# A graph layer on one core: the hand-made order of instructions is given up for the framework's scheduler

## The chip, the cores and the metric

The kernel runs on one NeuronCore of a Trainium2 chip. The metric is the device time of one launch in microseconds (us): the median of three runs, 1224.73 us (1222.9 to 1227.51). Five engines work side by side, each through its own list of instructions in order: PE (TensorE, matmuls, with PEld for its weight loads), DVE (VectorE), ACT (ScalarE), POOL (GpSimd) and SP (SyncE, which here only issues transfers). ACT and POOL issue transfers too, from the same lists.

## The reference, cut to what matters

```python
edge_index = jnp.stack([src, dst])               # 100000 edges, sorted by dst; 6250 nodes of 128 features
Xs = X[src]
m_data = Xs @ W_data.T + b_data
m_ctrl = Xs @ W_control.T + b_control
msg = jnp.where((edge_types == 0)[:, None], m_data, m_ctrl)
agg = jax.ops.segment_sum(msg, dst, num_segments=X.shape[0])
out = jax.nn.relu(agg + (X @ W_self.T + b_self))
x = _layernorm(x + out, axis=-1)
```

## The kernel before, in words

The nodes are cut into 49 blocks of 128. `sums_over_windows` works in three stretches.

**Build** (`messages`, lines 270 to 302). Seven groups of seven blocks. A group's inputs come in one transfer `xt_sb` (line 276, 448 KB, issued by ACT, two buffers). Each block has one float32 matmul with the three weight matrices (line 284) and one that adds the bias (285), into one of three PSUM buffers `g_ps`. ACT and DVE split the two kinds of message into three bfloat16 parts each (lines 289, 291, 292; POOL makes the last, 293), and ACT copies the node's own term (290). At a group's end ACT issues the store of `own` (296) and two stores of `table` (299). The messages also stay in SBUF as `m3`.

**Places** (`place(grp)`, lines 377 to 555), once for each of six groups of five blocks. For 18 steps k DVE writes one-hot tiles `hot_st` (434, five instructions of 128 columns, nine buffers), PE counts with them (438, matrix `tri`), DVE reads the slot (441), PE closes the count (445, matrix `rest`); every third step DVE makes `hr` and `two` (415, 418) and PE scatters them (426). Then come short chains (469 to 554) and one POOL gather `msg_s` (538). The result is written to DRAM as `packed` (458) and read back, spread over all partitions, as `rows` (368), one for each block.

**Sums.** For 30 of the blocks, `packed_sums` (563 to 608) runs 25 ticks each. A tick is one quad, four matmuls of 32 weight columns each into `g_ps` (line 581; their weights are `rows`, made ready by DVE at 561); a one-hot `hot_p` from DVE (584, four buffers); a cast `gs` from ACT (587, four buffers); and, two ticks later (`LAG`), one matmul that adds the tick to `agg_p` (590). A block ends with one more matmul (594), four DVE steps on its sums (`finish`, 88 to 91), and each fifth block with the layer norm (`norm_and_store`, 99 to 129: some twenty DVE steps, one ACT square root, one store). For the other 19 blocks `gathered` (320 to 362) fetches each edge's message by POOL (337, six at a time, six buffers `msg`), DVE writes a one-hot `hot` (354, four buffers) and PE adds (355, `agg_g`); the end of a block is `finish` and, each fifth time, the layer norm.

What sets the order: `manual_schedule()` (line 148) keeps each engine's list in the order in which the program was written. That order is made by the driver at lines 611 to 637: `place(0)` is stepped three times for each build block from the 15th on; then each tick of `packed_sums` is followed by a step of the next `place`, and by as many steps of `gathered` as spread its 342 tiles over the 750 ticks. Buffers and the waits on them come from the tile pools in either case.

Of the kernel before, what the change touches and what calls it, by code (L numbers as in the profile page):

```python
# [46 lines left out]
def kernel(  # L47
# [83 lines left out]
    with ExitStack() as main:  # L131
        sums_over_windows(main, tc, x, xt, edges, w, bias, table, own, packed, total,
                          finish, load_rows, norm_and_store)
# [6 lines left out]
def sums_over_windows(ctx, tc, x, xt, edges, w, bias, table, own, packed, total,  # L140
# [4 lines left out]
    work = ctx.enter_context(tc.tile_pool(name="work", bufs=2))  # L145
    ps_g = ctx.enter_context(tc.tile_pool(name="ps_g", bufs=3, space=PSUM))
    ps_a = ctx.enter_context(tc.tile_pool(name="ps_a", bufs=1, space=PSUM))
    ctx.enter_context(tc.manual_schedule())


    r0 = const.tile([EC, 1], I32, name="r0")
# [597 lines left out]
```

## Time and profile before

| what | value |
|---|---|
| median of the runs | 1224.73 us |
| profiled execution, its own time | 1234.9 us |
| its span, first to last instruction | 1233.2 us |
| PE busy | 804.8 us (65%) |
| DVE busy | 664.2 us (54%) |
| ACT busy | 405.3 us (33%) |
| POOL busy | 371.7 us (30%) |
| mean granted clock of PE | 0.718 |

All terms further on come from the profiled execution, which is 0.8% above the median. A row of the profile names the line of the program, the engine, the operation, `out<-in` and the number of instructions; a bracket at its end is the time that the engine stood idle just before, and what released it. [...]

### The profile page before, as it was taken

The numbers are of one execution on the slowest core, as the hardware profiler recorded it, in microseconds if no ns is written. First come the engines' busy times: TensorE is split into PE (matmuls) and PEld (weight loads), VectorE is DVE, ScalarE is ACT, GpSimd is POOL, SyncE is SP. The second block draws the span as 40 slices with busy tenths as digits, with TensorE's granted clock in tenths as the row PEclk, the third lists the DMA queues.
The fourth block names the chain that finished last, engine by engine and source line by source line (L and its number), as shares of the span: only waits on it lengthen the run. The fifth ranks groups of instructions, "written<-read, shape, count | busy, mean of one in ns | idle before, by whom it ended". The sixth has DMA issues, their size and how long they took to land.

```text
span 1233.2 us, 16402 instructions
## 1 busy us (share of the span) xinstructions
PE 804.8 (65%) x5211; PEld 253.3 (21%) x5211; DVE 664.2 (54%) x2722; ACT 405.3 (33%) x921; POOL 371.7 (30%) x405
## 2 busy tenths in 40 slices
PE   4454454534777657677677766677776777567784
PEld 1111121101222112222122221222222222112221
DVE  3043440413665456666576655676657666544455
ACT  2211112212333333333343333334343334234462
POOL 2110111272333233243332334314333332233400
PEclk9555555556777578786697777868768787577896
DMA  2512204431111132112231121322123211232200
GB/s 53 148 30 75 75 7 128 154 105 44 59 60 41 65 119 67 49 45 86 87 102 54 39 76 40 107 74 66 43 77 115 74 61 28 78 108 81 83 1 21
DMA packets 72192, 86.87 MB, mean 70 GB/s; under 512 B 18534, under 2 KB 61843, under 8 KB 72051
## 3 DMA queue, kind: packets, MB, share of 16 engines
q0 software_dynamic: 16736, 34.26, 10.0%
q1 hardware_dynamic: 35054, 35.26, 8.9%
q10 hardware_dynamic: 20310, 16.26, 4.4%
q8 instruction: 41, 0.67, 0.2%
q14 instruction: 51, 0.42, 0.1%
HBM read 69.51 MB, written 16.23 MB: 70 GB/s over the span
## 4 chain that ended last, share of the span: by engine, by line
PE 32%; issue 27%; DVE 15%; POOL 14%; DMA 6%; another core or an unknown queue 2%; ACT 2%; ACTq 0%; POOLq 0%; DVEq 0%
POOL msg L337 14%; PE g_ps L581 9%; PE agg_p L590 9%; PE g_ps L284 5%; PE agg_g L355 4%; DMA xt_sb<-in_xt 4%; DVE hot_st L434 2%; PE g_ps L285 2%; PE acc L438 2%; DVE s L90 1%; DVE two L418 1%; DVE hot_p L584 1%; DMA msg<-table,idx 1%; DVE r L291 1%
## 5 line engine op out<-in xcount | busy, mean ns | idle before, releaser
L587 ACT CAST gs<-g_ps 128x384 bf16<-128x384 f32 (+1 forms) x750 | 351.9, 480 | 581.6 <-PE g_ps L581 408.4
L337 POOL DMA_INDIRECT msg<-table,idx x342 | 331.3, 969 | 536.1 <-PE agg_g L355 436.6
L590 PE MATMUL agg_p<-gs,hot_p 128*128 128x384 bf16 (+1 forms) x750 | 297.7, 397 | 124.2 <-issue 76.2
L584 DVE TENSOR_SCALAR hot_p<-iota_b,to 128x128 bf16<-128x128 bf16 (+1 forms) x750 | 188.9, 262 | 270.1 <-PE agg_p L590 120.7
L581 PE MATMUL g_ps<-m,rows 128*32 128x384 bf16 x2940 | 306.4, 399 | 6.2 <-DVE rows L561 6.2
L355 PE MATMUL agg_g<-msg,hot 128*128 128x384 bf16 x342 | 137.8, 406 | 137.9 <-DVE hot L354 107.2
L581 PEld LDWEIGHTS <-rows 128*32 128x32 bf16 x2940 | 78.7, 96 | 286.4 <-issue 276.6
L284 PE MATMUL g_ps<-w_sb,xt_sb 128*128 128x384 f32 x98 | 76.5, 883 | 60.0 <-DMA xt_sb<-in_xt 60.0
L434 DVE TENSOR_SCALAR hot_st<-iota_b,st 128x128 bf16<-128x128 bf16 x540 | 112.2, 266 | 0.0
L590 PEld LDWEIGHTS <-hot_p 128*128 128x128 bf16 (+1 forms) x750 | 73.5, 98 | 176.1 <-issue 172.3
L441 DVE TENSOR_REDUCE slot<-acc 128x5 f32<-128x490 f32 x108 | 71.9, 666 | 50.1 <-PE acc L438 32.3
L438 PE MATMUL acc<-hot_st,tri 128*128 128x490 bf16 x108 | 52.0, 481 | 65.0 <-DVE hot_st L434 56.3
L291 DVE TENSOR_TENSOR r<-g_ps,m 128x256 f32<-128x256 f32 x49 | 20.8, 424 | 134.0 <-ACT own_sb L290 134.0
L293 POOL TENSOR_TENSOR m<-r,m 128x256 bf16<-128x256 f32 x49 | 32.8, 669 | 194.2 <-ACT m L292 194.2
L354 DVE TENSOR_SCALAR hot<-iota_b,rel 128x128 bf16<-128x128 bf16 x342 | 88.0, 258 | 0.2
L355 PEld LDWEIGHTS <-hot 128*128 128x128 bf16 x342 | 35.6, 104 | 235.3 <-DVE hot L354 177.5
L289 ACT CAST m<-g_ps 128x256 bf16<-128x256 f32 x49 | 18.2, 372 | 143.5 <-PE g_ps L285 143.4
L561 DVE TENSOR_SCALAR rows<-rows,pid 128x800 bf16<-128x800 bf16 x120 | 50.2, 421 | 0.6 <-DMA xs<-in_x 0.6
L445 PE MATMUL acc<-hot_st,rest 128*128 128x490 bf16 x108 | 49.6, 460 | 1.1 <-DVE slot L441 1.1
L284 PEld LDWEIGHTS g_ps<-w_sb,xt_sb 128*128 128x128 f32 x98 | 25.4, 305 | 105.6 <-issue 90.3
L426 PEld LDWEIGHTS <-hot_st 128*128 128x128 bf16 x540 | 37.5, 113 | 42.3 <-issue 35.2
L426 PE MATMUL small<-two,hot_st 128*128 128x64 bf16 x540 | 41.0, 216 | 3.3 <-DVE two L418 3.3
(135 smaller groups left out, 376.8 us busy)
## 6 DMA issues: line engine op xcount, KB each, us to landing
rows<-packed SPq DMA_DIRECT2D x30, 784.0 KB
table<-m ACTq DMA_DIRECT2D x14, 672.0 KB
msg<-table,idx POOLq DMA_INDIRECT x342
xt_sb<-in_xt ACTq DMA_DIRECT2D x7, 448.0 KB
own<-own_sb ACTq DMA_DIRECT2D x7, 448.0 KB
xs<-in_x SPq DMA_DIRECT2D x49, 64.0 KB
xs<-own SPq DMA_DIRECT2D x49, 64.0 KB
out<-h_p SPq DMA_DIRECT2D x6, 320.0 KB
```

What stands on the lines that cost most here:

```text
L284: T.matmul(y, xt_sb[:, j, :], w_sb, start=True, stop=False)
L337: G.indirect_dma_start(out=msgs[c][:, k, :], out_offset=None, in_=table[:, :], in_offset=bass.IndirectOffsetOnAxis(ap=idx[:, j, k0 + k : k ...
L354: V.tensor_scalar(hot, iota_b, rel[:, j, k0 + k : k0 + k + 1], None, op0=ALU.is_equal)
L355: T.matmul(agg, hot, msg[:, k, :], start=k0 + k == 0, stop=k0 + k == KT - 1)
L426: T.matmul(vt_v[:, q, :], hots[k][:, q, :], two[:, k - k0, q, :], start=k == 0 and q == 0, stop=k == KT - 1, skip_group_check=True)
L434: V.tensor_scalar(hot[:, q, :], iota1_b, st1[:, q, k : k + 1], None, op0=ALU.is_equal)
L438: T.matmul(acc_v, tri, hot[:, :, :NT], start=k == 0, stop=False, skip_group_check=True)
L441: V.tensor_reduce(slot[:, k, :], acc_v, axis=AX.X, op=ALU.max)
L581: T.matmul(g_ps[t * R : (t + 1) * R, :], sp[:, 4 * g + t, :], m3[:, 4 * g + t, :], start=True, stop=True)
L584: V.tensor_scalar(hot[: n * R], iota_b[: n * R], to[: n * R, q, g : g + 1], None, op0=ALU.is_equal)
L587: A.copy(gs[: n * R], g_ps[: n * R])
L590: T.matmul(agg, hot[: n * R], gs[: n * R], start=g == 0, stop=False)
```

## The change

One line goes; everything else is the same word for word.

```diff
     ps_a = ctx.enter_context(tc.tile_pool(name="ps_a", bufs=1, space=PSUM))
-    ctx.enter_context(tc.manual_schedule())
+
```

The same instructions with the same buffers are now put in order by the framework's scheduler: it plays the program through with its own table of durations, and lets each engine take, of the instructions whose inputs and buffers it takes to be ready, the one that stands first in the program. The lists differ in many places; three of them follow. In each, the first fence is the order before and the second the order now.

ACT, at the end of the build's first group. `xt_sb` is the transfer of a later group's inputs; `m` is `m3`, `r` is `r1`.

```order
L289 CAST m_347<-g_ps 128x2x128
L290 COPY own_sb<-g_ps 128x128
L292 CAST m_347<-r_425 128x2x128
L296 DMA own<-own_sb 128x7x128
L299 DMA table<-m_347 128x7x384 x2
L276 DMA xt_sb<-in_xt 128x896
L289 CAST m_347<-g_ps 128x2x128
```

```order
L292 CAST m_345<-r_405 128x2x128
L276 DMA xt_sb<-in_xt 128x896
L292 CAST m_345<-r_414 128x2x128
L289 CAST m_345<-g_ps 128x2x128
L290 COPY own_sb<-g_ps 128x128
L289 CAST m_345<-g_ps 128x2x128
L296 DMA own<-own_sb 128x7x128
```

Before, the second group's inputs are asked for behind the first group's stores. Now the first two groups' inputs are asked for at the start (two of these transfers stand in a row there), and the one shown is the third group's, ahead of the first group's stores.

DVE, where the first five packed blocks are normalised (103 to 119); `hot_p` is what PE needs for the next ticks.

```order
L104 BN_AGGR mv<-st 128x2
L107 TENSOR_SCALAR v<-mv 128x5
L111 RECIPROCAL r_3322<-s_3320 128x5
L113 TENSOR_TENSOR q<-v,r_3322 128x5
L114 TENSOR_TENSOR q<-q,s_3320 128x5
L116 RECIPROCAL rstd<-q 128x5
L117 TENSOR_SCALAR rstd<-rstd 128x5
L119 TENSOR_SCALAR h_p<-h_p,mv,rstd 128x128 x5
```

```order
L103 BN_STATS st<-h_p 128x6
L584 TENSOR_SCALAR hot_p<-iota_b,to 128x128
L104 BN_AGGR mv<-st 128x2
L584 TENSOR_SCALAR hot_p<-iota_b,to 128x128
L107 TENSOR_SCALAR v<-mv 128x5
L88 TENSOR_TENSOR s<-agg_g,xs 128x128
L584 TENSOR_SCALAR hot_p<-iota_b,to 128x128
L90 TENSOR_TENSOR s<-agg_g,s 128x128
L111 RECIPROCAL r_3320<-s_3318 128x5
```

The layer norm was one piece of DVE's list; now one-hots for PE, and another block's `finish`, stand between its steps.

PE, in a packed block beside which the next `place` runs. A quad is the four matmuls of line 581, each with its weight load.

```order
L590 MATMUL agg_p<-gs,hot_p 128x384
L355 LDWEIGHTS hot
L355 MATMUL agg_g<-msg,hot 128x384
L581 LDWEIGHTS rows
L581 MATMUL g_ps<-m_347,rows 32x384
L581 LDWEIGHTS rows
L581 MATMUL g_ps<-m_347,rows 32x384
L581 LDWEIGHTS rows
L581 MATMUL g_ps<-m_347,rows 32x384
L581 LDWEIGHTS rows
L581 MATMUL g_ps<-m_347,rows 32x384
L590 LDWEIGHTS hot_p
```

```order
L590 MATMUL agg_p<-gs,hot_p 128x384
L581 LDWEIGHTS rows
L581 MATMUL g_ps<-m_345,rows 32x384
L355 LDWEIGHTS hot
L355 MATMUL agg_g<-msg,hot 128x384
L581 LDWEIGHTS rows
L581 MATMUL g_ps<-m_345,rows 32x384
L581 LDWEIGHTS rows
L581 MATMUL g_ps<-m_345,rows 32x384
L581 LDWEIGHTS rows
L581 MATMUL g_ps<-m_345,rows 32x384
L590 LDWEIGHTS hot_p
```

Before, all 750 quads stand in one piece. Now 177 of them are cut by another matmul (166 once and 11 twice: 188 cuts), nearly all in the sixth to the 25th packed block, some nine a block. Counted over a block, PE's work has kept its place: at each end of a packed block as many tiles of `gathered` and steps of `place` lie behind PE as before, within five or so. One shift is larger: ten of the 18 steps of `place(1)` now stand inside the build, beside those of `place(0)`. POOL's list is the same, within six gathers.

## Rows read from the trace of the kernel before

**Rows 1.** The page: busy time of each engine, share of the span, instructions.

```profile
PE 804.8 (65%) x5211; PEld 253.3 (21%) x5211; DVE 664.2 (54%) x2722; ACT 405.3 (33%) x921; POOL 371.7 (30%) x405
```

**Rows 2.** Stretches of the build: us, busy times, granted clock (PEclk), DMA share, GB/s.

```profile
40.20:54.50 14.30, 14.09 (x21) 4.19 (x21) 2.55 (x6) 5.73 (x19) 3.41 (x6) 0.50 0.19 34
65.50:97.50 32.00, 19.00 (x46) 6.53 (x47) 17.53 (x57) 6.62 (x21) 4.33 (x7) 0.50 0.01 3
105.90:139.00 33.10, 20.38 (x63) 7.64 (x63) 17.57 (x48) 5.67 (x18) 4.00 (x6) 0.50 0.00 0
```

**Rows 3.** The page's costliest groups: busy, mean ns; idle before and its releaser.

```profile
L284 PE MATMUL g_ps<-w_sb,xt_sb 128*128 128x384 f32 x98 | 76.5, 883 | 60.0 <-DMA xt_sb<-in_xt 60.0
```

**Rows 4.** The build in order of time: start, us, instruction, idle before.

```profile
16.90 1.62 PE L284 MATMUL g_ps<-w_sb,xt_sb 128*128 128x384 f32 x2 [2.93 <-DMA xt_sb<-in_xt]
...
26.74 0.91 PE L284 MATMUL g_ps<-w_sb,xt_sb 128*128 128x384 f32 x2
...
27.84 0.91 PE L284 MATMUL g_ps<-w_sb,xt_sb 128*128 128x384 f32 x2
...
33.05 1.46 ACTq L276 DMA_DIRECT2D xt_sb<-in_xt  x1
...
40.31 1.62 PE L284 MATMUL g_ps<-w_sb,xt_sb 128*128 128x384 f32 x2 [11.29 <-DMA xt_sb<-in_xt]
...
77.67 0.57 PE L438 MATMUL acc<-hot_st,tri 128*128 128x490 bf16 x1 [1.85 <-DVE hot_st L434]
```

**Rows 5.** Between build and sums, in order of time.

```profile
243.91 1.44 DVE L561 TENSOR_SCALAR rows<-rows,pid 128x800 bf16<-128x800 bf16 x4 [0.64 <-DMA xs<-in_x]
...
285.72 0.48 ACT L587 CAST gs<-g_ps 128x384 bf16<-128x384 f32 x1 [14.91 <-remote]
```

**Rows 6.** Packed blocks from one line 594 to the next; columns as in rows 2.

```profile
341.77:375.21 33.44, 26.05 (x173) 8.23 (x173) 22.67 (x89) 11.68 (x26) 12.05 (x12) 0.74 0.15 46
...
636.37:672.33 35.96, 26.02 (x173) 7.95 (x172) 21.71 (x86) 11.58 (x26) 11.33 (x12) 0.76 0.19 59
...
1151.86:1176.50 24.64, 18.60 (x137) 5.56 (x137) 11.40 (x49) 11.66 (x26) 8.22 (x9) 0.86 0.26 82
1176.50:1194.73 18.23, 16.01 (x136) 5.37 (x136) 11.06 (x48) 11.97 (x26) 0.00 (x0) 1.00 0.01 1
```

**Rows 7.** PE's waits from 300 to 1200 us: in total, times, longest.

```profile
PE agg_g L355 <- DVE hot L354: 100.7, 70, 9.0
...
PE acc L438 <- DVE hot_st L434: 17.2, 9, 4.0
...
PE agg_g L355 <- DVE bad L551: 7.5, 1, 7.5
```

**Rows 8.** The first layer norm: its last step, and PE behind it.

```profile
445.80 1.37 DVE L119 TENSOR_SCALAR h_p<-h_p,mv,rstd 128x128 f32<-128x128 f32 x5
...
447.77 0.50 PE L355 MATMUL agg_g<-msg,hot 128*128 128x384 bf16 x1 [8.80 <-DVE hot L354]
```

**Rows 9.** PE's matmuls at the lower clock, then at the full one.

```profile
449.52 0.50 PE L590 MATMUL agg_p<-gs,hot_p 128*128 128x384 bf16 x1
...
449.81 0.53 PE L355 MATMUL agg_g<-msg,hot 128*128 128x384 bf16 x1
...
450.27 0.51 PE L581 MATMUL g_ps<-m,rows 128*32 128x384 bf16 x4
...
450.71 0.50 PE L590 MATMUL agg_p<-gs,hot_p 128*128 128x384 bf16 x1
...
1207.23 0.34 PE L590 MATMUL agg_p<-gs,hot_p 128*128 128x384 bf16 x1
...
1207.40 0.33 PE L355 MATMUL agg_g<-msg,hot 128*128 128x384 bf16 x1
...
1207.66 0.35 PE L581 MATMUL g_ps<-m,rows 128*32 128x384 bf16 x4
...
1207.94 0.34 PE L590 MATMUL agg_p<-gs,hot_p 128*128 128x384 bf16 x1
```

## The prediction

> **What bounds the kernel now.** I read the busy times first: no engine is near its span, and PE is the fullest at 65% [rows 1]. So the question in each stretch is for what PE waits, and the views of PE's idle time come next.
>
> In the build PE waits for transfers: 60.0 us ahead of the float32 matmuls, all put down to `xt_sb` [rows 3]. One row shows why: the second group's inputs are issued at 33.05, behind the first group's stores, and PE starts at 40.31 after 11.29 us of idleness [rows 4]. A group without `place` beside it is solid: 14.09 us busy of 14.30, so 2.04 us a block at a granted clock of 0.50 [rows 2]. A group with `place` beside it lasts 32 to 33 us with 19 to 20 busy [rows 2]: 13 us go in handing over between PE and DVE, as in the 1.85 us for `hot_st` [rows 4].
>
> In the sums the views by packed block say most. A late block without `place` takes 24.64 us while POOL gathers and 18.23 when POOL is done [rows 6]: some 6.4 us of a block go with the gathers, whatever the order (in the first long burst a cast on ACT stood still for 14.91 us [rows 5]). With `place` beside it a block takes 33 to 36, and PE is busy for 26 [rows 6]. So in these blocks PE's own list, with a fifth of the time lost to the gathers, is what ends last; DVE has 22 us of work there. The waits of PE that an order can cure are those for DVE: 100.7 + 17.2 + 7.5 = 125.4 us [rows 7]. Seven of them, of 6.9 to 9.0 us (the longest 9.0 [rows 7]), stand at a layer norm and come to 56 us; the first, 8.80 us, ends as the normalisation's last steps are through [rows 8].
>
> **The change, part by part**, against the profiled execution's 1234.9 us (span 1233.2, 1.7 outside).
>
> *Transfers of the build.* Each group's inputs are now asked for while the group before is computed, 14 us or more for a transfer that takes 7 (33.05 to 40.31 [rows 4]). Of the 60.0 us the first wait, 2.93, before any work, stays [rows 4]: **-57**. The cover is a whole group on PE; if it were gone the 57 would be back.
>
> *`place` in the build.* Ten more steps k stand there. Two groups with six steps each have 19.00 and 20.38 us of PE against 14.09 in one without [rows 2], so 0.93 us a step: **+9**. The handovers cost 13 us in each of these groups (32.00 - 19.00, 33.10 - 20.38 [rows 2]) and the same in a third, 39 us for 18 steps or 2.2 a step. Now `hot_st` is written ahead, which takes most of the 1.85 us away, but 14 of the 28 counts have their second half right behind them and wait for DVE's reduction. I take 1.25 a step, 35 in place of 39: **-4**. Bounds: 62, if each of 28 steps kept 2.2; 14, if only the 14 waits of about a microsecond were left.
>
> So the build ends 52 us sooner. Behind it nothing is new: the last store, `rows`, its selection (first at 243.91 [rows 5]) and the 36 gathers follow each other as before.
>
> *Steps of `place(1)` gone from the sums.* A block with six steps takes 33.44, one without 24.64 [rows 6], so 1.47 us a step; ten: **-14**.
>
> *Layer norms.* With one-hots for PE between its steps, PE goes on while DVE normalises, though more slowly, since DVE's work is as much as before. I take three quarters of 56: **-42** (bounds -25 and -56).
>
> *Shorter waits for DVE.* 125.4 less 56 leaves 69 us, many of them short and behind a block's `finish`. `finish` too is now mixed with one-hots. I take a good third: **-26** (0 to -50).
>
> *Cut quads.* This is what the change costs. From one matmul of full width to the next PE goes in 0.29 us at the lower clock (449.52 to 449.81) and 0.17 at the full one (1207.23 to 1207.40); into a quad or out of it the step is 0.44 to 0.46 and 0.26 to 0.28 [rows 9]. In the order sum, tile, quad, sum this makes 0.29 + 0.46 + 0.44 = 1.19 us, or 0.71; in the order sum, one, tile, three, sum there are four steps into or out of a quad's width: 1.80, or 1.08. A cut costs 0.6 us at the lower clock and 0.37 at the full one. These blocks run at 0.74 to 0.76 [rows 6], half way, so 0.48; 188 cuts: 91 us. A quarter of it should fall into the time that the gathers take from PE anyway: **+68** (bounds +20, if most is hidden, and +113, all at the lower clock).
>
> [...]
>
> Sum: -57 + 9 - 4 - 14 - 42 - 26 + 68 = -66, so 1168.9 us in that execution. The median is 0.8% below the profiled one (1224.73 / 1234.9 = 0.992), which makes **1159 us**, 5% faster. With the bounds of the single terms moved against each other, this case reaches from 1115 to 1203.
>
> **Rivals**, in the same scale.
>
> *PE's clock rises in the build.* In the first group the float32 matmuls went from 1.62 to 0.91 us after ten microseconds of work, one block each 1.10 us [rows 4]; a later group, as solid and 14 us long, stayed at 0.50 [rows 2]. Without the pauses the full clock may come and stay: 42 blocks save up to 0.94 us each, less what ACT's casts then hold back, some 33 us: 1169 - 33 = 1136, so 1127. Against it: that second group. [...]
>
> *The cuts are hidden.* If PE is not what ends last in the blocks with `place`, a cut costs little: +20 in place of +68, 1121, so 1112. For it: PE is idle for 7 to 10 us in such a block [rows 6]. Against it: 6.4 of these go with the gathers.
>
> *The norms' waits come back.* DVE has the same work, and a one-hot that now stands behind some other late step makes PE wait in turn. If none of the 68 us (42 + 26) is gained, the sum is +2, 1237, and the time 1227: no change.
>
> *Slower.* The cut quads cost more than the slots. ACT casts a quad only when its fourth matmul is through, so a cut delays the cast (0.48 us long [rows 5]) and the sum that waits for it. The gains come to 134 us (57 - 9 + 4 + 14 + 42 + 26), so the change turns at 0.71 us a cut. At the lower clock a cut with the cast's length on top is 0.6 + 0.48 = 1.08; three quarters of 188 x 1.08 are 152, the sum is +18, 1253, so 1243. For it: casts and sums stand only two ticks apart, with three PSUM buffers. Against it: most quads stay whole in a third of the blocks, and two ticks are a microsecond or more.
>
> That the order does not change is excluded by the lists themselves.
>
> **How the numbers follow.** 0.5% is about what a measurement of this kernel can tell from no change: 6 us, from 1218.6 to 1230.9. Chances: forecast (1115 to 1203) 0.47; clock rises (1127) 0.15; cuts hidden (1112) 0.15; waits come back (1227) 0.09; slower (1243) 0.14. Faster 0.47 + 0.15 + 0.15 = 0.77, same 0.09, slower 0.14. The range goes from 1088, since the two fast rivals can meet, to 1232, which leaves out the slower case and a little at the low end.
>
> **What would show it.** Build: idle time for `xt_sb` near 3 us in place of 60, the first selection of `rows` near 192 us in place of 243.91 [rows 5], at a granted clock near 0.5 before it. Sums: PE's waits of over 6 us for `hot` gone, those for DVE together near 57 in place of 125; packed blocks with a norm at 32 to 34 us, the blocks from the sixth to the 25th without one 2 to 3 us longer than before, the first three near 25; the last six unchanged. The forecast is wrong if blocks with nine cuts take no longer, if they take over 5 us longer, or if that first selection moves by less than 35 or more than 75 us.

## The result, and the profile after

The changed kernel takes 1065.43 us (median; 1047.55 to 1071.72), the kernel before 1226.12 us beside it: a ratio of 0.859, with a 95% interval from 0.846 to 0.872, some 14% faster. The ratio leaves out two of the four runs, over 1.5% longer than the shortest, of which the profiled one is one; with them the medians give 0.869. The forecast was 1159 us with a range from 1088 to 1232, so the direction was right and the time lies below the range. The profiled execution took 1071.72 us.

First the page of the changed kernel: span, busy times, the granted clock in 40 slices.

```profile
span 1070.0 us, 16296 instructions
...
PE 794.8 (74%) x5211; PEld 255.0 (24%) x5211; DVE 623.9 (58%) x2722; ACT 397.0 (37%) x921; POOL 371.8 (35%) x405
...
PEclk9986555568867997886988869898688788588788
```

PE is busy for 795 us, 10 less than in [rows 1]. What fell is its idle time, from 428 us (1233.2 - 804.8) to 275. By stage, in the two traces, with the first selection of `rows` and the lines 594 as marks:

| stage | before | after | change |
|---|---|---|---|
| start to first selection of `rows` | 243.9 | 163.1 | -80.8 |
| from there to the end of the first packed block | 65.0 | 64.2 | -0.8 |
| the 29 other packed blocks | 903.6 | 829.1 | -74.5 |
| behind the last of them | 20.7 | 13.7 | -7.0 |

The forecast had -52 for the first row and -14 for the rest. The build as a whole, from its first float32 matmul to its last (columns as in rows 2), of the kernel before:

```profile
16.90:231.50 214.60, 115.78 (x275) 38.57 (x276) 69.27 (x188) 45.46 (x145) 31.60 (x48) 0.55 0.25 71
```

and of the changed one:

```profile
20.80:151.30 130.50, 117.95 (x341) 39.20 (x342) 90.98 (x289) 42.30 (x145) 32.06 (x47) 0.73 0.40 116
```

PE has 66 more matmuls there and is idle for 12.5 us in place of 98.8. The records of the granted clock, a share of full speed, hold two values in these two traces, 0.50 and 1.00. In the kernel before it is 0.50 from 447 to 452 us, where the first half of [rows 9] lies, and 1.00 from 1206 to 1208, where the second lies. The granted clock of the two rows here (0.55 and 0.73) does not show a rise. The clock's record begins only 26 us after the start in the first trace and 63 us in the second, and the profile counts what lies ahead of it as full clock, here and in PEclk. In the changed kernel:

```profile
20.80:63.00 42.20, 39.76 (x78) 12.35 (x79) 24.54 (x82) 12.99 (x45) 9.34 (x14) 1.00 0.40 111
```

and in that stretch the float32 matmuls of a block took

```profile
22.79 1.65 PE L284 MATMUL g_ps<-w_sb,xt_sb 128*128 128x384 f32 x2
```

which is their length at the lower level (1.62 us in [rows 4], where the other is 0.91). Of the 49 blocks of the build 4 took under 1 us for them, 3 in the kernel before: by these lengths the build ran at the lower clock both times, for the most part. The page's group that answers to [rows 3]:

```profile
L284 PE MATMUL g_ps<-w_sb,xt_sb 128*128 128x384 f32 x98 | 76.1, 878 | 5.2 <-DMA xt_sb<-in_xt 3.2 <-DVE r L291 2.0
```

The largest of PE's waits from 20.8 to 151.3 us:

```profile
PE acc L445 <- DVE slot L441: 9.6, 13, 1.0
```

In the sums the waits have changed their kind. PE's waits of the changed kernel over the whole span (in total, times, longest):

```profile
PE g_ps L581 <- ACT gs L587: 61.3, 54, 4.0
PE agg_p L590 <- ACT gs L587: 53.0, 29, 14.2
PE agg_p L590 <- issue: 48.4, 27, 11.0
PE g_ps L581 <- issue: 35.0, 32, 3.2
PE acc L445 <- DVE slot L441: 18.8, 24, 2.3
PE agg_p L590 <- DVE hot_p L584: 9.9, 11, 2.0
...
PE agg_g L355 <- DVE hot L354: 3.2, 4, 2.2
```

The 100.7 us for `hot` of [rows 7] are 3.2 now. In their place stand waits for casts and waits that the profile puts down to nothing, 198 us together against 137 before. One of them in order of time, ACT's row and then PE's:

```profile
217.99 0.48 ACT L587 CAST gs<-g_ps 128x384 bf16<-128x384 f32 x1 [14.92 <-remote]
...
218.52 0.48 PE L590 MATMUL agg_p<-gs,hot_p 128*128 128x384 bf16 x1 [14.16 <-ACT gs L587]
```

It is the kind of stall of [rows 5], in the first long burst of gathers, with PE behind it. These stalls turned out to be the main thing to understand in the experiments: with the kernel itself unchanged, they are there at some times and not at others. The kernels of one set were timed on one chip together with the kernel before, and every ratio below is against it: it took 1255 and 1258 us in two sets (and 1226 above), 1028 to 1032 us in four. Chip number 10 gave 1032 in one set and 1258 in another, so "a chip with the stalls", as the expectations say, should read "a set of runs with the stalls".

### The profile page after: what moved, and what is told of

The parts are those of the page before. It is cut to its first block, busy times and chain, and to the rows that moved or that the text cites. A ratio compares the mean times of both kernels' runs of the same rounds, so it can differ in the third digit from the quotient of the medians.

```text
span 1070.0 us, 16296 instructions
## 1 busy us (share of the span) xinstructions
PE 794.8 (74%) x5211; PEld 255.0 (24%) x5211; DVE 623.9 (58%) x2722; ACT 397.0 (37%) x921; POOL 371.8 (35%) x405
## 4 chain that ended last, share of the span: by engine, by line
PE 68%; another core or an unknown queue 10%; issue 7%; DVE 7%; ACT 5%; DMA 2%; ACTq 0%; DVEq 0%; SPq 0%
PE g_ps L581 25%; PE agg_p L590 19%; PE agg_g L355 7%; PE g_ps L284 6%; ACT gs L587 5%; PE acc L438 3%; PE acc L445 3%; PE small L426 2%; PE g_ps L285 2%; DVE slot L441 2%; DVE hot_st L434 1%; PE agg_p L594 1%; DVE hot_p L584 1%; DVE two L418 1%
## 5 line engine op out<-in xcount | busy, mean ns | idle before, releaser
L587 ACT CAST gs<-g_ps 128x384 bf16<-128x384 f32 (+1 forms) x750 | 347.0, 480 | 541.4 <-PE g_ps L581 220.6
L581 PE MATMUL g_ps<-m,rows 128*32 128x384 bf16 x2940 | 328.1, 388 | 99.7 <-ACT gs L587 61.3
L590 PE MATMUL agg_p<-gs,hot_p 128*128 128x384 bf16 (+1 forms) x750 | 281.5, 388 | 114.7 <-ACT gs L587 53.0
L584 DVE TENSOR_SCALAR hot_p<-iota_b,to 128x128 bf16<-128x128 bf16 (+1 forms) x750 | 193.8, 266 | 216.0 <-PE agg_p L590 100.0
L581 PEld LDWEIGHTS <-rows 128*32 128x32 bf16 x2940 | 83.3, 96 | 358.5 <-issue 355.2
L355 PE MATMUL agg_g<-msg,hot 128*128 128x384 bf16 x342 | 132.7, 391 | 3.2 <-DVE hot L354 3.2
L434 DVE TENSOR_SCALAR hot_st<-iota_b,st 128x128 bf16<-128x128 bf16 x540 | 117.8, 268 | 0.0
L289 ACT CAST m<-g_ps 128x256 bf16<-128x256 f32 x49 | 18.3, 373 | 52.2 <-PE g_ps L285 52.2
L426 PE MATMUL small<-two,hot_st 128*128 128x64 bf16 x540 | 35.5, 211 | 1.0 <-DVE two L418 0.7
L426 PEld LDWEIGHTS <-hot_st 128*128 128x128 bf16 x540 | 28.5, 109 | 20.9 <-issue 17.6
L292 ACT CAST m<-r 128x256 bf16<-128x256 f32 x49 | 18.9, 408 | 38.0 <-DVE r L291 31.5
L291 DVE TENSOR_TENSOR r<-g_ps,m 128x256 f32<-128x256 f32 x49 | 19.3, 416 | 20.2 <-ACT own_sb L290 18.3
```

Of the source, the lines that this page charges most:

```text
L355: T.matmul(agg, hot, msg[:, k, :], start=k0 + k == 0, stop=k0 + k == KT - 1)
L426: T.matmul(vt_v[:, q, :], hots[k][:, q, :], two[:, k - k0, q, :], start=k == 0 and q == 0, stop=k == KT - 1, skip_group_check=True)
L434: V.tensor_scalar(hot[:, q, :], iota1_b, st1[:, q, k : k + 1], None, op0=ALU.is_equal)
L581: T.matmul(g_ps[t * R : (t + 1) * R, :], sp[:, 4 * g + t, :], m3[:, 4 * g + t, :], start=True, stop=True)
L584: V.tensor_scalar(hot[: n * R], iota_b[: n * R], to[: n * R, q, g : g + 1], None, op0=ALU.is_equal)
L587: A.copy(gs[: n * R], g_ps[: n * R])
```

## The experiments

### One stage at a time

**prefetch**: the written order, and only `xt_sb` asked for one group ahead.

```
             xt_next = load(0)
             for g in range(NB // GN):
-                xt_sb = ... A.dma_start(xt_sb, ...)
+                xt_sb, xt_next = xt_next, load(g + 1)
```

> The written order, with one thing changed: each group's xt_sb is asked for one group ahead. If the forecast's first term is right and independent of the rest (the 60 us of waiting for xt_sb go, 3 stay, and nothing else moves), the time falls by 57 us, the first selection of rows comes near 187 us, and the granted clock over the build stays near 0.55. Rival: PE's pauses also held its clock down, so a solid build is faster in itself: the time falls by 70 us or more, the clock of the build is above 0.62 and the float32 matmuls take less. Second rival: the wait turns into another (casts, r1, stores): the time falls by less than 40 us.

Measured: 1199.79 against 1255.27 us, ratio 0.957 (0.952 to 0.962), so -55.5. The first selection came at 193.6 us, 50 us earlier than in the trace of the kernel before. The group of the float32 matmuls, and what PE waited for up to 240 us (two views):

```profile
L290 PE MATMUL g_ps<-w_sb,xt_sb 128*128 128x384 f32 x98 | 78.5, 904 | 3.5 <-DMA xt_sb<-in_xt 3.4
```

```profile
PE acc L444 <- DVE hot_st L440: 42.2, 18, 6.7
```

The first term of the forecast stands by itself, as expected: the wait did not turn into another, the matmuls were no faster (904 ns), and the 42 us for `hot_st` stayed.

**sched_build** and **sched_sums**: the scheduler orders the build alone, or everything from the first gathers on alone.

```
-    ctx.enter_context(tc.manual_schedule())
     ...
     for _ in slots:
         pass
+    ctx.enter_context(tc.manual_schedule())      # sched_build; sched_sums: left here, entered above
     stream = gathered()
```

> The scheduler orders the build, the written order stays for everything from the first gathers on. PE's list in the sums is the written one. If the two stages add up, the time falls by what the first selection of rows moved in the changed kernel, 81 us, and it is near 1145; the sums last as long as in the kernel before. Rival: part of the gain of the build came from the ten steps of place(1) that no longer can be moved there (then the build is some 9 us shorter still, 90 us), or the build's higher clock carries into the sums (more than 95 us).

> The reverse: the written order in the build, the scheduler from the first gathers on. If the stages add up, the time falls by 82 us less what the ten steps of place(1) are worth that stay in the sums (14 us at 1.47 each), so by 68 to 82 us. By the forecast's own sums (norms -42, waits -26, cuts +68) it would not change at all: 0 to +5 us. The number of changes between quarter and full width in PE's list is 1307 here, 1495 as written.

Measured: sched_build 1156.72 us, ratio 0.920 (0.913 to 0.926), -98.5; sched_sums 1184.09 us, ratio 0.944 (0.939 to 0.949), -71.2. The two shares, 8.0% and 5.6%, add to 13.6%; the whole change gave 14.1%. So the stages add up. In sched_build the first selection came at 150.6 us, 12.5 earlier than in the changed kernel, where ten steps of `place(1)` stand in the build as well. The forecast had +9 for them. Part of the 12.5 is the clock: 13 of the 49 float32 blocks took under 1 us here, 4 in the changed kernel, and at some 0.7 us a block that makes an estimated 6.5 us. And the sums did gain, where the forecast's own terms of them (-42, -26, +68) came to nothing.

**prefetch_dve**: as prefetch, with DVE's list alone freed in the build; PE, ACT, POOL and SP keep theirs.

> The written order with xt_sb asked for one group ahead, and in the build DVE's list alone the scheduler's; PE keeps the written list there. In the run named prefetch PE still waits 42 us for hot_st, and the first selection of rows comes at 193.6 us. If the waits go because DVE writes hot_st ahead, whatever PE's order, the selection comes near 155 us and the time falls by 40 us more (ratio 0.92 on a chip where prefetch gave 0.957). If it takes PE's freed order too, hot_st's waits stay above 25 us and the selection comes after 180 us. The forecast's own term (4 us of 39) would put it at 190.

Measured: 937.32 against 1032.22 us, ratio 0.909 (0.905 to 0.913), -95; the first selection at 147.5 us (244.5 in a trace of the kernel before from another set). PE's waits up to 240 us:

```profile
PE g_ps L292 <- DVE r L299: 15.8, 9, 3.7
...
PE acc L446 <- DVE hot_st L442: 3.0, 2, 1.9
PE acc L453 <- DVE slot L449: 1.5, 2, 1.2
```

With DVE working ahead the wait for `hot_st` falls from 42.2 us (prefetch) to 3.0; PE's freed order is not needed. The waits for `slot`, which the forecast had kept for 14 counts, are 1.5 us in this kernel, with PE's order as written, and 9.6 in the build of the changed one. The clock has a part in the earlier selection too: 20 of the 49 float32 blocks took under 1 us, none in prefetch, an estimated 14 us. The 15.8 us for `r` are new: DVE is late with the build's own subtraction in turn.

### What a cut quad costs

**cut**: the written order, with the stream's step drawn behind the first matmul of a quad in place of behind the sum.

```
                 for t in range(n):
                     T.matmul(g_ps[t * R : (t + 1) * R, :], sp[:, 4 * g + t, :], ...)
+                    if t == 0:
+                        yield 1          # the gathered tile's step is drawn here
             ...                          # the driver's lines for it are left out
```

> The written order, with each gathered matmul of agg_g put behind the first matmul of the next quad where it stood behind the sum: 335 quads are cut, and the changes of width in PE's list rise from 1495 to 2165. By the forecast (0.48 us a cut at this clock, three quarters of it on the path) the time rises by 335 x 0.36 = 121 us. If cuts are hidden, as the rival had it (20 us for 188), it rises by 36 us or less. If a cut also holds back the cast (0.71 us or more each), it rises by over 200 us.

Measured: 1312.19 against 1255.27 us, ratio 1.046 (1.041 to 1.052), +57, or 0.17 us a cut: between the two. The page of this kernel, beside [rows 1]:

```profile
PE 922.2 (71%) x5211; PEld 293.4 (23%) x5211; DVE 667.7 (51%) x2722; ACT 403.7 (31%) x921; POOL 370.9 (29%) x405
```

PE is busy for 117 us more (922.2 - 804.8), 0.35 a cut, for which the forecast had 0.48. PE's idle time is 379 us against 428 in the trace of before (of another set): part of the price fell into waits that were there anyway. The forecast put three quarters of it on the path, and it was 0.17 of 0.35, about half. What a cut consists of stands in order of time, at the full clock by the length of a sum (0.34 us, as in the second half of [rows 9]):

```profile
1144.51 0.34 PE L581 MATMUL g_ps<-m,rows 128*32 128x384 bf16 x1
1144.78 0.34 PE L355 MATMUL agg_g<-msg,hot 128*128 128x384 bf16 x1
1145.04 0.34 PE L581 MATMUL g_ps<-m,rows 128*32 128x384 bf16 x3
1145.32 0.34 PE L592 MATMUL agg_p<-gs,hot_p 128*128 128x384 bf16 x1
```

One matmul of a quad holds PE for 0.27 us, the three others for 0.28, and a whole quad for 0.28 as well [rows 9]. So a cut adds more than two changes of width: each piece takes as long as a whole quad.

**join**: two quads, then their two sums, in the written order.

```
-                if len(todo) > LAG:
+                while (b * NS + g) % 2 == 1 and len(todo) > LAG:
                     todo.pop(0)()
```

> The written order, with the sums of agg_p in pairs: two quads, then two sums. The changes of width fall from 1495 to 1221, and sums that directly follow a sum rise from 31 to 405. If a change of width costs 0.10 us at the full clock and 0.15 at the lower one, PE's busy time falls by 27 to 41 us and the time by about half of it, 12 to 20 us. Rival: a sum behind a sum into the same accumulator takes as long as one behind a quad (0.26 us against 0.28 at the full clock, in the changed kernel), so nothing is saved: PE's busy time stays within 10 us, and the time does not fall.

Measured: 1074.98 against 1032.03 us, ratio 1.042 (1.038 to 1.045): slower, by 43 us, which neither theory had. PE is busy for 731.3 us, 725.6 in the kernel before in another set without the stalls, at a mean granted clock of 0.763 against 0.793, and its waits for DVE come to 242 us against 203. Its busy time is within the 10 us that the rival gave; the rival's reason falls all the same. In the changed kernel, where PE works without stalls (run after_2, in order of time):

```profile
300.42 0.49 PE L590 MATMUL agg_p<-gs,hot_p 128*128 128x384 bf16 x2
...
304.69 0.38 PE L438 MATMUL acc<-hot_st,tri 128*128 128x490 bf16 x1
304.91 0.32 PE L355 MATMUL agg_g<-msg,hot 128*128 128x384 bf16 x1
305.07 0.49 PE L590 MATMUL agg_p<-gs,hot_p 128*128 128x384 bf16 x2
305.49 0.51 PE L581 MATMUL g_ps<-m,rows 128*32 128x384 bf16 x8
305.93 0.38 PE L445 MATMUL acc<-hot_st,rest 128*128 128x490 bf16 x1
```

Two sums take 0.49 us where one takes 0.34, so the second follows after some 0.15; two quads in a row (x8) hold PE for 0.44 us (305.49 to 305.93) where one holds it for 0.28 [rows 9]. Into another width the step is 0.26 to 0.28 us at the full clock [rows 9], so each change of width that is avoided is worth an estimated 0.1 us there. In this run nothing of it reached the time, since the waits for DVE grew; why they did is not settled.

### Which engine's list pays in the sums

**sums_dve** and **sums_pe**: the written order in the build, and in the sums on all engines but one.

```
+    ctx.enter_context(tc.manual_schedule(engines={SP, mybir.EngineType.PE, mybir.EngineType.Activation,
+                                                  mybir.EngineType.Pool}))    # sums_pe: DVE for PE
     stream = gathered()
```

> Written order in the build and, in the sums, on every engine but DVE; the scheduler orders DVE's list alone there. PE's list keeps its 1495 changes of width (1497). By the forecast the gain of the sums is DVE's (layer norms -42, shorter waits -26, nothing lost to cuts): the time falls by about 68 us, and PE's waits for hot fall from 100 to 40 us or less. Rival: the gain of the sums (71 us with all engines free) is PE's own list, and DVE's order alone brings under 25 us.

> Written order in the build and, in the sums, on every engine but PE; the scheduler orders PE's list alone there. It has 1103 changes of width in place of 1495, though many quads are cut. By the forecast's one-sided price (cuts only) the time rises. If what counts is the number of changes, 392 fewer at 0.10 to 0.15 us each take 39 to 59 us off PE's own work, of which something under a half shows, as in the run with cut quads (57 us of 131): the time falls by 17 to 26 us, and PE's waits for hot stay near 100 us unless PE now has other work there. Third: PE's list alone brings all of it, 60 us or more.

Measured, in a set of runs without the stalls: sums_dve 846.83 against 1032.03 us, ratio 0.820 (0.815 to 0.824); sums_pe 934.23 us, ratio 0.903 (0.899 to 0.908). PE's waits of sums_dve in the sums:

```profile
PE agg_g L356 <- DVE hot L355: 14.8, 23, 2.6
```

and of sums_pe:

```profile
PE g_ps L582 <- ACT gs L588: 58.5, 116, 4.4
...
PE agg_g L356 <- DVE hot L355: 15.2, 16, 6.4
```

Either list, freed alone, cures most of the waits for `hot` (116.1 us in the kernel before without the stalls, shown below), and both gain more than was expected (185 and 98 us). PE's has a price that DVE's does not have. In sums_pe PE waits 58.5 us for casts (2.8 in sums_dve), since each quad needs one of the three PSUM buffers that ACT's casts free, and it is busy for 702.7 us against 665.3, although it changes width 1103 times in place of 1495. The number of changes alone does not give PE's time.

**build_and_dve** and **build_and_pe_kept** free the build, and in the sums DVE alone, or everything but PE. **after_2** is the changed kernel beside them, **sums_dve_2** a repeat.

> The changed kernel itself once more, beside the next three and on the same chip, since two chips gave the kernel before 1255 and 1032 us. If its gain is a share of the time, the ratio is 0.86 again. If the stalls that the first traces show while POOL gathers are the chip's (the chip with 1032 us shows hardly any), and the scheduler's order hides part of them, the gain is smaller on a chip without them: 0.88 to 0.92 there.

> The scheduler orders the build, as in the changed kernel, and in the sums DVE's list alone; PE, ACT, POOL and SP keep the written order there, and PE its 1495 changes of width with no quad cut. If the scheduler's cut and moved quads cost PE time, as the forecast had it, this kernel is faster than the changed one: at the forecast's 68 us by some 6%, ratio to before 0.76 to 0.82. Rival: PE's list as the scheduler orders it is no worse than the written one, and the kernel is within 2% of the changed one or slower.

> As the run before, but in the sums only PE keeps the written order; DVE, ACT, POOL and SP are the scheduler's. If PE's list is what makes the difference between the changed kernel and the run before, this one equals the run before within 1.5%. If it is ACT's, POOL's or SP's order (casts, gathers, loads), it equals the changed kernel.

> The kernel with only DVE's list free in the sums once more, on the chip of the three others. If DVE's order is what pays in the sums, it is faster than before by 14 to 18%, and the run with the build added is faster by a further 7 to 9% (81 to 98 us of the build). If the 18% belonged to the other chip, it is under 10% here.

Measured, against 1028.29 us, again without the stalls: after_2 758.97 us (ratio 0.737, 0.731 to 0.742), build_and_dve 750.67 (0.731, 0.726 to 0.736), build_and_pe_kept 745.43 (0.720, 0.713 to 0.728), sums_dve_2 846.45 (0.823). The build is worth 9.2% here (0.823 less 0.731). The change itself gains 26%, not the 8 to 12% that were expected: with the stalls there about half of that was left. Against build_and_pe_kept PE's freed order costs 17 us (the ratios' difference, 0.0164 of 1028; 7 to 26 by their intervals), and it is a cost, as the forecast had it, but a quarter of its 68. build_and_dve lies between the two, within 2% of after_2. Of PE's time 25.5 us more are busy (675.9 and 650.4) and 8.4 fewer idle. Its largest groups, of after_2

```profile
L581 PE MATMUL g_ps<-m,rows 128*32 128x384 bf16 x2940 | 281.8, 338 | 20.6 <-ACT gs L587 15.0 <-DVE rows L561 2.8 <-issue 0.5
L590 PE MATMUL agg_p<-gs,hot_p 128*128 128x384 bf16 (+1 forms) x750 | 242.0, 335 | 6.9 <-DVE hot_p L584 4.1 <-DVE mv L104 1.1 <-ACT gs L587 0.7
```

and of build_and_pe_kept:

```profile
L580 PE MATMUL g_ps<-m,rows 128*32 128x384 bf16 x2940 | 261.9, 340 | 12.6 <-DVE rows L560 12.6
L589 PE MATMUL agg_p<-gs,hot_p 128*128 128x384 bf16 (+1 forms) x750 | 254.0, 339 | 0.0
```

The quads take 19.9 us more, the sums 12 less (matmuls in flight at once count in both groups: a sum's record of 0.34 us runs on when the next matmul starts 0.17 us behind it [rows 9]). That fits the steps: a single matmul of a quad holds PE for 0.27 us and the three others for 0.28, where the whole takes 0.28, and a sum behind a sum takes 0.15.

### The stalls

**before_2**, **build_and_pe_kept_2** and **after_3** repeat three kernels; **no_gather** keeps the written order and 30 of the 342 gathers, so the sums of the gathered blocks are left out in effect.

```
-            if c < len(chunks):
+            if MSG_BUFS - 1 <= c < len(chunks):
+                msgs[c] = kept[c % (MSG_BUFS - 1)]
+            elif c < len(chunks):
```

> The kernel before itself, for its trace on the chip of the next three. On a chip with the stalls (1220 to 1260 us) PE's idle time that no program rule explains (waits put down to nothing, to a remote releaser or to casts that had stood still) is 120 us or more in the sums; on one without them (about 1030 us) it is under 20, and PE's waits are those for DVE: 150 us or more for hot, hot_st and bad together, which is more than the 125 of the first trace, since DVE no longer catches up while PE stands still.

> The scheduler orders everything but PE's list in the sums, which stays as written (1495 changes of width, no quad cut). On a chip without the stalls this gave 0.720 of the time before. On a chip with them: by the forecast's cut term (68 us, 5.5%) it is faster than the changed kernel by 4 to 6%; if PE's free order saves what it cuts by what it joins, by no more than 2%; if PE's free order fills the stalls, the changed kernel is faster by 2% or more.

> The changed kernel on the chip of these four: 0.86 of the time before on a chip with the stalls, 0.74 on one without them.

> The written order with 30 of the 342 gathers of msg: the later matmuls of agg_g read the first five tiles of msg again, so the sums of the gathered blocks are left out in effect, and every instruction of PE, ACT and DVE stays. If the stalls come with the gathers, then on a chip with them the time falls by 120 to 250 us, to near what a chip without them gives (about 1030), and PE's waits with no releaser nearly vanish; on a chip without them nothing changes by more than 2%. If the stalls have another cause (the clock, the profile, other transfers), the time falls by less than 50 us on a chip with them.

This set too was without the stalls: before 1031.71 us, before_2 1028.03, build_and_pe_kept_2 746.18 (ratio 0.724, 0.720 to 0.728), after_3 764.33 (0.739, 0.733 to 0.746), no_gather 1019.77 (0.991, 0.987 to 0.995). PE's freed order costs 15 us here, again by the ratios (8 to 23). before_2 gives the trace of the kernel before without the stalls; of its page the clock, and PE's waits:

```profile
PEclk9655555555979779898799977978878899789896
```

```profile
PE agg_g L355 <- DVE hot L354: 116.1, 88, 7.7
PE g_ps L284 <- DMA xt_sb<-in_xt: 61.2, 7, 11.8
PE acc L438 <- DVE hot_st L434: 59.5, 31, 3.4
```

No wait without a reason of the program is left. In after_2 PE's waits for `hot` and `hot_st` come to 2.9 us, its longest wait in the sums is under 3 us, and from 170 us on the digits of its clock stand at 9 up to the last (the first two digits lie ahead of the clock's record, as does the first of before_2):

```profile
PEclk9976565559999999999999999999999999999997
```

From before_2 to after_2 PE's idle time falls from 297.1 to 83.6 us and its busy time, at a mean granted clock of 0.922 for 0.793, from 725.6 to 675.9. With the stalls it was 428 to 275, and 805 to 795.

**build_and_pe_kept_3** and **no_gather_2**: the same two kernels once more.

> The scheduler orders everything but PE's list in the sums. On a chip with the stalls (before at 1220 to 1260 us) the forecast's cut term (68 us) gives a ratio of 0.80 to 0.82 against the changed kernel's 0.859; if joined quads make up for cut ones, 0.845 to 0.86; if PE's free order is what fills the stalls, above 0.87. On a chip without them 0.72 again.

> The written order with 30 of the 342 gathers of msg, the others left out (the gathered blocks are then summed from the wrong rows). On a chip with the stalls: if they come with the gathers, the time falls to 1010 to 1060 us and PE's idle time without a program's reason nearly vanishes; if not, it falls by less than 50 us. On a chip without them it is 0.99 of the time before again.

This set had the stalls (before 1258.09 us). no_gather_2 took 1059.03 us, ratio 0.843 (0.835 to 0.851): 199 us less, with PE's waits

```profile
PE agg_g L357 <- DVE hot L356: 124.5, 91, 7.7
PE acc L440 <- DVE hot_st L436: 66.6, 33, 6.0
...
PE agg_p L592 <- ACT gs L589: 14.4, 2, 12.4
PE agg_p L592 <- issue: 12.1, 3, 7.1
```

The stalls come with the gathers, or with the transfers that go with them: beside the 30 left PE still waits 26 us in this way, and from the second packed block on each block lasts what it lasts in before_2 (23.8, 27.6, 23.4 us against 24.8, 27.8, 23.4). build_and_pe_kept_3 took 1055.70 us, ratio 0.839 (0.835 to 0.843), of which PE still waited

```profile
PE agg_p L589 <- issue: 110.5, 56, 14.9
PE agg_p L589 <- ACT gs L586: 71.7, 52, 5.9
PE agg_g L354 <- DVE hot L353: 17.8, 17, 2.6
```

It is 2% below the changed kernel's 0.859, which by 1226 us is 24 us, from 8 to 41 by the two intervals (the two ratios come from different sets of runs), and lies between the two ranges that were expected. In all three comparisons build_and_pe_kept is faster than the changed kernel.

## Why the prediction was wrong, point by point

**Transfers (-57): right.** 55.5 us measured alone; the wait is 3.2 us in the changed kernel, as said.

**`place` in the build: near for the ten steps (12.5 us against 9, part of it the clock), wrong for the handovers.** The step that failed is "I take 1.25 a step, 35 in place of 39". PE's whole idle time in the build is 12.5 us now, less than the lower bound of 14. What is left is what that bound named: 13 waits for `slot`, 9.6 us together. The other 21 of the 35 us did not come: no wait for `hot_st` is left in the build, and prefetch_dve shows the cause, DVE's list, which alone brings it from 42.2 to 3.0 us. sched_build gained 43 us over prefetch (98.5 - 55.5), an estimated 9 of them by the clock (13 float32 blocks under 1 us against none, 0.7 us each). At the forecast's 1.25 a step its 18 steps would have gained 16.5 (39 less 22.5).

**Norms and waits for DVE (-42 and -26): right in kind, too small.** PE's waits for `hot` fell from 100.7 us [rows 7] to 3.2, the longest from 9.0 to 2.2, and DVE's waits in the sums stand at some 23 in place of the 57 that were forecast. With PE's list as written and the stalls there, the sums' share is 104 us (build_and_pe_kept_3's 202.4 less sched_build's 98.5), near the sum of the two upper bounds, 106. The forecast doubted that DVE, with the same work, could be ahead in more than three quarters of the norms. It is busy for 58% of the span, and with its list free PE's longest wait for `hot` is 2.2 us. In the traces without the stalls the same shows with DVE's list freed alone: 14.8 us for `hot` in sums_dve against 116.1 in before_2.

**Cut quads (+68): right in sign, wrong in size.** The price of a cut on PE was near (0.35 for 0.48; at the full clock sum, one, tile, three, sum takes 0.26 + 0.27 + 0.26 + 0.28 = 1.07 us by the rows of the run cut and [rows 9], against 0.71 uncut, so 0.36 for the forecast's 0.37). Two steps failed. First the count was one-sided: of the changed list 177 quads are cut, but 266 stand directly behind the quad before, two in the kernel before. Such a join saves two changes of width, 0.23 us at the full clock (0.28 + 0.26 less 0.16 and 0.15). An estimate by these steps is 188 x 0.37 - 264 x 0.23, some +9 us in place of +68. Changes of width alone would mislead the other way: they fall, from 1495 to 1343, and yet PE's order costs time, since a cut also adds a piece that takes as long as a quad. Then three quarters on the path were too many: 0.17 of 0.35 in the run named cut. What PE's freed order costs in all is 17 and 15 us without the stalls and 24 (8 to 41) with them; the ten steps of `place(1)` that it moves to the build are in it. Had the forecast been right, the blocks from the sixth to the 25th, but for those with a norm, would have been 2 to 3 us longer than before; the mean of the 13 of them in which no wait of over 6 us stood before fell from 31.6 to 30.4 us. The steps of the traces show the change of width by itself: 0.28 us for a quad behind a sum, 0.16 for one behind a quad.

**The whole.** Had each of these terms been taken at the favourable bound that the prediction itself named (14 for the handovers, -56, -50, +20), the sum would have been -57 + 9 - 25 - 14 - 56 - 50 + 20 = -173, and (1234.9 - 173) x 0.992 = 1053 us, 12 below the measured median. The range treated the bounds as if they moved against each other. They moved together. Three of them have one cause, which the runs show: DVE, freed, runs ahead of PE in the build (prefetch_dve) and in the sums (sums_dve). The fourth, the cuts, came out low for the reasons above. The -14 for the steps of `place(1)` that leave the sums was not measured by itself.

**Rivals.** PE's clock in the build: refuted here. Without the pauses it stayed at the lower level but for 4 of the 49 float32 blocks (3 before), and these matmuls took 878 ns in place of 883 [rows 3]; the forecast's "near 0.5" was right. In prefetch_dve and sched_build they took 739 and 812, because 20 and 13 blocks took under 1 us; what decides which level is granted is open. PE was busy for 118 us of 130.5 here and these matmuls were no faster, while in after_2 the digits of the clock stand at 9 from 170 us on. Cuts hidden: nearest to what was seen, with 15 to 24 us against its 20. Waits come back: in part, and from ACT instead of DVE, 198 us of casts and unexplained waits against 137. In after_2, without the stalls, 16 us of these are left, so that most of them are the stalls; that they had lain under DVE's waits before is likely, but not shown. Slower: refuted; a cut costs 0.17 us on the path, not 0.71.

**Smaller misses.** The first float32 matmul starts 3.9 us later (20.81 for 16.90), and the end behind the last block is 7 us shorter; neither was forecast. The last two blocks went from 18.2 and 17.7 to 16.0 and 15.2 us; they had been called unchanged. The first three behind the first, which should have come near 25, took 27.4, 28.4 and 31.1. And "some 6.4 us of a block go with the gathers, whatever the order" belongs to the stalls, not to the kernel: the block of 24.64 us of [rows 6] lasts 21.0 in before_2, with its gathers, and 21.0 in no_gather_2, without them; the one ahead of it went from 24.8 to 18.3 and 18.4.

## What to carry to other kernels

When an order is changed, count what is joined as well as what is cut, and ask for every bound of the sum which cause would bring it: bounds with one cause come together, and the range has to hold their sum. Where a trace shows waits that no instruction explains, find out whether they are the kernel's before building on them, since they can hide a part of the gain (14% with them here, 26% without). A cut cost what its pieces took here (0.27 and 0.28 us where the whole quad takes 0.28), not only the change of width. Here the best order kept PE's list in the sums, written by hand, and left the engine that feeds it free to run ahead.

## What the chip showed that was not expected

While POOL issued row gathers, PE's and ACT's instructions stood still for up to 15 us at a time with nothing in the program to wait for, in some sets of runs and not in others, on the same chip (number 10): 1258 us against 1032 for the same kernel, 1056 against 746 for the best one. With 30 of 342 gathers the longer time fell to 1059 us. What differs between the sets no run shows.

The granted clock was lower beside the stalls too. In the changed kernel's first packed block, with the stalls, then without (columns as in rows 2):

```profile
163.11:227.27 64.16, 23.54 (x138) 5.95 (x138) 15.41 (x63) 12.32 (x27) 35.59 (x38) 0.53 0.27 84
```

```profile
160.90:179.63 18.73, 18.18 (x137) 5.41 (x138) 14.85 (x63) 12.34 (x27) 10.98 (x12) 0.76 0.37 112
```

The same 137 or 138 matmuls take PE 23.5 us at a granted clock of 0.53 and 18.2 at 0.76, and the block 64 us or 19: with the stalls PE's own work was 5.4 us longer.
